# Two graph layers on one core: the third hop computed in seven products, its weights applied behind it, and the tests of the matrix moved into layer 0's norm

## The chip, the cores and the metric

The kernel runs on one core of one Trainium2 chip. The metric is the device time of one execution in microseconds (us). Before the change it is 839.94 us, the median of three runs (839.57 to 840.18).

A core has a matrix engine, TensorE (PE), that multiplies a loaded 128-row block of weights (the first operand, `lhsT`) by columns that stream past it (`rhs`) and adds up in PSUM; it has VectorE (DVE), ScalarE (ACT) and GpSimd (POOL) for elementwise work between PSUM and SBUF, and SyncE (SP), which here only issues transfers (DMA). Each engine runs its own queue of instructions in order; semaphores join them.

## What is computed

```python
# x: (8, 2048, 64), adj: (2048, 2048): a symmetric 0/1 pattern with ones on the
# diagonal and about 0.4% of the rest set, each row divided by its sum
def layer0(x, A, embedding, weight, bias):            # D = 16, K = 3
    w = jnp.einsum('nd,dkio->nkio', embedding, weight)   # weights of each node
    b = jnp.einsum('nd,do->no', embedding, bias)
    As = [I, A, 2.0 * (A @ A) - I]
    x_g = jnp.einsum('knm,bmc->bnkc', jnp.stack(As, 0), x)
    return jnp.einsum('bnki,nkio->bno', x_g, w) + b
def layer1(x0, A, weight, bias):                      # both supports are adj
    x1 = A x0;  x2 = 2.0 * (A x1) - x0
    return concat([x0, x1, x2, x1, x2]) @ weight + bias  # weight: (320, 64)
x = layernorm(x + layer0(x, adj, ...))
x = layernorm(x + layer1(x, adj, adj, ...))
```

So the large work is four multiplications of the 2048 x 2048 matrix by 2048 x 512 features (8 batches of 64 channels), called hops here: two in layer 0, two in layer 1.

## The kernel before

**Tiles.** The 2048 nodes are NT = 16 tiles of P = 128. A tile of features is 128 x 512 (`z[s][t]`). `z[0]` holds x, later layer 0's output h; `z[1]` and `z[2]` hold what the hops give and what they add to.

**The matrix as a pattern.** Every row of `adj` has one value wherever it is not zero. The hops therefore multiply the 0/1 pattern [...]and scale the result by that value (`rcol`, `rrow`). A slab is 128 rows of `adj`, loaded by `slab` (L191) on SP's queue, which carries the loads in program order into RAW = 5 rotating buffers `raw`; `places` (L196) makes the pattern on DVE. `places_equal` (L201) makes it too, and counts in the same instruction (L205) how many elements equal the row's value. `check` (L648) compares that count with the count of elements that are not zero (L445, an ACT copy `seen` with an accumulator, in the first hop); if they differ, `general`, a kernel for any matrix, computes the output in place of this one. Features are split in two fp32r parts, `high` (L208, ACT) and `low` (L211, DVE), so every product is two matmuls.

**First hop** (`hop_x`, L396; about 6 to 122 us). 512 matmuls of 512 columns (L229). `put_together` (L386) makes sums of quarters of the pattern on the side and POOL's queue writes them to DRAM (`sums_of`, L394).

**Second hop** (`seven_products`, L460; to 225 us). Seven products of half-size matrices in place of eight, with those sums: 7 x 8 steps of 8 matmuls of 512 columns, 448 in all (L529). The features are the loaded operand and the pattern streams past, so the result comes out transposed, into `z2`, by `put` (L545). Where a product needs a plain quarter of the pattern, it is loaded as a slab and made by `places`; products 2 to 4 read `sums_of`.

**Layer 0's mixing** (L623 to L640; 226 to 593 us). For each tile `mix0` (L321) has eight groups of 12 matmuls `pm` (L342); DVE adds each group into `acc`, scaled by the node's embedding, with four instructions of 128 x 256 (L348). `layernorm` (L303) follows: sum over channels (L306) and times 1/64 (L307) on DVE, subtraction on POOL (L309, `xc`), squares on ACT (L300), their sums on DVE (L301), `rsqrt` (L278), and the product on POOL (L312). `project` (L353) multiplies the transposed h by three 64 x 64 weights `v` (L361, 192 columns at a time), copies two of the results with ACT (L368) and adds the bias to the third with DVE (L369). The loop overlaps tiles: ahead of tile t's last group, `between` (L628) transposes h of tile t - 1 (L268, L270), prepares tile t + 1's operands (a load of `xt`, and transposes) and scales tile t + 2 (`times_r`, POOL); `project` of tile t - 1 stands behind tile t's groups.

**Third hop** (`hop_h`, L600; 593 to about 711 us). Pattern times h, after the projection: 16 slabs for 4, 8 and 4 tiles, 512 matmuls (L229), each slab made by `places_equal`, so that the whole matrix is tested here; results are scaled and added to `z[1]` by `evict` (L252), whose weights h already carries through `project`.

**Fourth hop** (`hop_g`, L675, and `hop_tile`, L697). Pattern times `z[1]`: the first eight tiles together, slab by slab in the order `ks`, then tiles 8 to 15 one by one, each normalised and stored (L318, L319) as it ends. PE ends at 826.9 us.

**What sets the order.** PSUM is one pool of four buffers of two banks each (`bank`, L81), which all of the above take in turn; a matmul into a buffer waits for the last reader of what was there four takings ago. Instructions wrapped in `ordered` keep the program's order while `in_order` is set, which it is during the first two hops and from the middle of the third hop's beginning on; elsewhere, in the mixing stage above all, a scheduler places them by readiness. `run` (L236) takes a list of steps, each made of parts with a lead (operands two steps ahead of their use, and so on), and pops two entries of `todo` (evictions and the like) per step.

Of the kernel before, what the change touches and what calls it, by code (L numbers as in the profile page):

```python
# [37 lines left out]
def pattern(  # L38
# [20 lines left out]

    nc = tc.nc  # L60
# [13 lines left out]
    rowpool = pool(hops, "frow", 1, side="right")  # L74
    hpool = pool(hops, "fhl", HL, side="right")
# [37 lines left out]
    v = const.tile([P, 3, C], F32, tag="v", name="v")  # L113
# [122 lines left out]
    def run(steps):  # L236

        got = [{} for _ in steps]
        for i in range(-6, len(steps)):
            for ahead in range(6, -1, -1):  # L240
                for lead, part in steps[i + ahead] if 0 <= i + ahead < len(steps) else ():
                    if lead == ahead:
                        part(got[i + ahead])
            for _ in range(2):
                if todo and i >= 0:
                    todo.pop(0)()
# [15 lines left out]
    def transpose(src, tag, pt=None):  # L262

        pt = bank("pt") if pt is None else pt
        for j in range(B // 2):
            for h in range(2):
                q = slice(h * C, (h + 1) * C)
                nc.tensor.transpose(pt[:, h, j * C : (j + 1) * C], src[q, 2 * j * C : 2 * (j + 1) * C], ident[q, q])  # L268
        tt = work2.tile([P, B // 2, P], F32, tag=tag, name=tag)
        nc.scalar.copy(  # L270
            tt.rearrange("p j (h n) -> p h j n", h=2), pt[:, :, : B // 2 * C].rearrange("p h (j n) -> p h j n", n=C)
        )
        return tt
# [4 lines left out]
    def rsqrt(ss):  # L278


        def col(name):
            return (work if ss.shape[1] == B else keep).tile(list(ss.shape), F32, tag=f"{name}{ss.shape[1]}", name=name)

        va = col("ln_v")
        nc.vector.scalar_tensor_tensor(va, ss, 1.0 / C, eps.to_broadcast(list(ss.shape)), ALU.mult, ALU.add)
        sd = col("ln_sd")
        nc.scalar.activation(sd, ss, AF.Sqrt, bias=eps, scale=1.0 / C)  # L287
        r0 = col("ln_r0")
        nc.vector.reciprocal(r0, sd)

        q = col("ln_q")
        nc.vector.scalar_tensor_tensor(q, r0, -0.5, r0, ALU.mult, ALU.mult)
        nc.vector.tensor_tensor(q, q, va, ALU.mult)
        r = col("ln_r")
        nc.vector.scalar_tensor_tensor(r, q, 1.5, r0, ALU.add, ALU.mult)
        return r

    def square_sums(src, to):
        sq = work.tile([P, B, C], F32, tag="ln_sq", name="sq")
        nc.scalar.activation(sq, src, AF.Square)  # L300
        nc.vector.tensor_reduce(to, sq, AX.X, ALU.add)  # L301

    def layernorm(src):  # L303

        s = work.tile([P, B], F32, tag="ln_s", name="s")
        nc.vector.tensor_reduce(s, src, AX.X, ALU.add)  # L306
        nc.vector.tensor_tensor(s, s, part, ALU.mult)  # L307
        xc = xcpool.tile([P, B, C], F32, tag="ln_xc", name="xc")
        nc.gpsimd.tensor_tensor(xc, src, wide(s), ALU.subtract)  # L309
        ss = work.tile([P, B], F32, tag="ln_ss", name="ss")  # L310
        square_sums(xc, ss)
        nc.gpsimd.tensor_tensor(xc, xc, wide(rsqrt(ss)), ALU.mult)  # L312
        return xc
# [7 lines left out]
    def mix0(t, tt, between):  # L321
# [4 lines left out]
        for g in range(2):  # L326
            part = acc[:, 4 * g : 4 * g + 4, :]
            nc.gpsimd.tensor_tensor(  # L328
# [3 lines left out]
            )  # L332
            for dg in range(D // DG):
                if g == 1 and dg == D // DG - 1:
                    between()
# [10 lines left out]
                for d in range(DG):  # L346
                    dd = dg * DG + d
                    nc.vector.scalar_tensor_tensor(  # L348
                        part, pm[:, :, :, d, :].rearrange("p j i c -> p (j i) c"), emb_sb[:, t, dd : dd + 1], part, ALU.mult, ALU.add
                    )  # L350
        return layernorm(acc)

    def project(t, hT, pus=None):  # L353


        for g in range(2):
            pm = bank("pu") if pus is None else pus[g]
            for i in range(2):
                for j in range(2):
                    q = slice(j * C, (j + 1) * C)  # L360
                    nc.tensor.matmul(  # L361
                        pm[:, j, i * 3 * C : (i + 1) * 3 * C], lhsT=hT[q, 2 * g + i, :], rhs=v[q],
                        start=True, stop=True,
                    )
            got = pm[:, :, : 6 * C].rearrange("p j (i k c) -> p j i k c", i=2, k=3)
            bs = slice(4 * g, 4 * g + 4)
            for s in range(2):
                nc.scalar.copy(bc(s, t)[:, bs, :].rearrange("p (i j) c -> p j i c", j=2), got[:, :, :, 2 - s, :])  # L368
            nc.vector.tensor_tensor(  # L369
                bc(2, t)[:, bs, :].rearrange("p (i j) c -> p j i c", j=2), got[:, :, :, 0, :],  # L370
                bias1.unsqueeze(1).unsqueeze(1).to_broadcast([P, 2, 2, C]), ALU.add,
            )
# [10 lines left out]
    S1, S2, S4, S3 = range(4)  # L383
    couple = []
# [11 lines left out]
    def hop_x(g, kk, j):  # L396
# [37 lines left out]
        def use(got):  # L434
# [10 lines left out]
            ordered(nc.scalar.activation(seen, s, AF.Copy, accum_out=nonzero[:, i : i + 1]))  # L445
            if last and g == 1:
# [13 lines left out]
    def seven_products(s, to, more):  # L460
# [3 lines left out]
        sums, kept = [], {}  # L464

        def sum_of_y(kk, name):
# [11 lines left out]
            if name == "T2":  # L478
# [4 lines left out]
                return add(y, add(y, quarter(2, 2), quarter(1, 2), ALU.subtract), quarter(1, 1), ALU.add)  # L483
            y = xcpool.tile([P, BC], F32, tag="ln_xc", name="y")
            if name == "T4":
                return add(y, kept[kk // 2][:, kk % 2], quarter(2, 1), ALU.subtract)
# [3 lines left out]
        def step(p, kk):  # L490
# [5 lines left out]
            def y_high(got):  # L496
                hl = hpool.tile([P, 2, BC], F32R, tag="hl", name="hl")
                got["hl"] = [hl[:, 0], hl[:, 1]]
                if name[0] == "B":
                    sum_y(got)  # L500
# [5 lines left out]
            def load_sum(got):  # L506
                if isinstance(which, tuple):
                    return
                raw = got["raw"] = rawp.tile([P, 2, Q], BF16, tag="raw", name="raw")
                load(nc.sync, raw, sums_of[kk, :, :, which, :].rearrange("g m n -> m g n"))  # L510

            def operands(got):
                if isinstance(which, tuple):
                    got["s"] = places(slab(kk + KK * which[1], which[0] * HALF, HALF))
# [7 lines left out]
            def use(got):  # L522
# [10 lines left out]
                if p == 0 and kk == 3:  # L533
                    node_bias(sums[1])
                    todo.extend(lambda h=h: keep_node_bias(sums[1], h) for h in range(2))
                if kk < KK - 1:
                    return
                if p < 6:
                    todo.extend([lambda: None] * 4)
                for i in range(2):  # L540
                    for c in range(2):
                        todo.append(lambda i=i, c=c: put(acc[i][:, c], i, c))
                todo.extend(more.get(p, ()))
# [21 lines left out]
            before = [(5, sum_y)] if name[0] != "B" else []  # L565
# [8 lines left out]
    def times_r(t):  # L574
# [6 lines left out]
    pieces = weights()  # L581
    more = {
        1: [lambda: ordered(next(pieces)) for _ in range(13)],
        5: [lambda: times_r(0), lambda: times_r(1)],
    }
    run([hop_x(g, kk, j) for g in range(2) for kk in range(KK) for j in range(2)] + seven_products(1, to_z2, more))
# [13 lines left out]
    def hop_h(g, first, n, k):  # L600
        def operands(got):
            if g == 0 and k == NT - 1:
                project(mixed[0], transpose(mixed[1].rearrange("p b c -> p (b c)"), "hT"))
                layer0.close()
                in_order.append(True)
            i = g * NT + k
            raw = slab(k, first * P, n * P)
            got["s"], got["hl"] = places_equal(raw, first * P, equal[:, i : i + 1]), halves(z[0][k])

        def use(got):  # L610
            s, hl = got["s"], got["hl"]
            if k == 0:
                accs[:] = banks(n)
            add_block(accs, s, hl, k == 0, k == NT - 1)
            if k == NT - 1:
                for i, a in enumerate(accs):
                    evict(z[1][first + i], first + i, a, i % 2)

        return [(2, operands), (0, use)]

    third = [hop_h(g, first, n, k) for g, (first, n) in enumerate(((0, 4), (8, 8), (4, 4))) for k in range(NT)]

    mixed = None  # L623
    tt = operands(0)
    for t in range(NT):
        done = {}

        def between():  # L628
            if mixed is not None:
                done["hT"] = transpose(mixed[1].rearrange("p b c -> p (b c)"), "hT")  # L630
# [5 lines left out]
        new = t, mix0(t, tt, between)  # L636
        tt = done.get("tt")
        if mixed is not None:
            project(mixed[0], done["hT"])
        mixed = new  # L640
# [7 lines left out]
    def check():  # L648
# [3 lines left out]
        tc.keep_in_program_order(nc.vector.tensor_tensor(bad, count("n_nz", nonzero), count("n_eq", equal), ALU.not_equal))  # L652
# [15 lines left out]
    EARLY = 8  # L668
    late = []
    ks = [0, 1, 2, 3, 8, 9, 10, 11, 12, 13, 14, 15, 4, 5, 6, 7]  # L670
    hls = {}
    sums = keep.tile([P, 8, B], F32, tag="sums", name="sums")
    late_values = {}

    def hop_g(k):  # L675
        def operands(got):
            i = ks.index(k)
            if i == EARLY:
                hops.close()
            if i in (0, EARLY):  # L680
                late.append(pool(ctx, f"flate{i}", 1, reuse_waits="tile"))
            got["s"] = places(slab(k, 0, HALF))
# [3 lines left out]
        def use(got):  # L686
            s, hl = got["s"], hls[k]
            if k == ks[0]:
                accs[:] = banks(8)
            add_block(accs, s, hl, k == ks[0], k == ks[-1])  # L690
            if k == ks[-1]:
                for t, a in enumerate(accs):
                    evict(z[2][t], t, a, t % 2)

        return [(2, operands), (0, use)]

    def hop_tile(t, c):  # L697
        def operands(got):
# [3 lines left out]
            got["s"] = places(raw)  # L702

        def use(got):
# [13 lines left out]
            for o in (2 * t - 16, 2 * t - 15):  # L718
                if o < 8:
                    square_sums(bc(2, o), sums[:, o, :])  # L720
            if t == 11:
                late_values["scales"] = rsqrt(sums.rearrange("p t b -> p (t b)"))
            if t >= 12:
                for o in (2 * t - 24, 2 * t - 23):
# [9 lines left out]
    run(third + [hop_g(k) for k in ks] + [hop_tile(t, c) for t in range(8, NT) for c in range(2)])  # L734
# [324 lines left out]
```

## Time and profile before

| what | before |
|---|---|
| median of 3 runs | 839.94 us |
| the profiled execution | 839.63 us |
| its span (first to last instruction) | 837.6 us |
| granted PE clock, mean | 0.994 |
| busy: PE, DVE, ACT, POOL | 823.5, 607.0, 224.6, 128.8 us |
| moved by DMA | 96.55 MB, 115 GB/s in the mean |

The page in front of all gives each engine's busy time and share of the span. Below it the span is cut into 40 equal slices, whose digits are busy tenths (9 is 90% or more). Then come the chain of work that ended last, followed back from the last instruction, and the costliest groups of instructions: line, engine, operation, result and operands by the program's names, shape, count; behind the bar the busy time, the mean of one in ns, and the idle time ahead of them with what ended most of it. A timeline lists one engine's instructions as start, duration (both us), engine, line, operation, operands, shape, count of a run of equal ones, and in brackets an idle time ahead and what ended it. PE's weight loads (PEld) are listed apart from its matmuls, which they overlap.

### The profile page before, as it was taken

How to read it: one execution, taken by the hardware profiler on the slowest of the kernel's cores; microseconds unless marked ns; L12 is line 12 of the kernel's file. 1: busy time of each engine (PE TensorE's matmuls, PEld its weight loads, DVE VectorE, ACT ScalarE, POOL GpSimd, SP SyncE). 2: the span in 40 equal slices, each digit the busy share in tenths (PEclk: the TensorE clock that was granted, in tenths of full speed). 3: DMA queues.
4: the chain of work that ended last, by engine and by line, in shares of the span. 5: the costliest groups of instructions: out<-in, count | busy, mean ns of one | idle time of the engine just before them, and what ended most of it. 6: DMA issues, size and time to landing. Idle time of an engine off the chain costs nothing.

```text
span 837.6 us, 14392 instructions
## 1 busy us (share of the span) xinstructions
PE 823.5 (98%) x5614; PEld 732.0 (87%) x5614; DVE 607.0 (72%) x1256; ACT 224.6 (27%) x427; POOL 128.8 (15%) x130
## 2 busy tenths in 40 slices
PE   9999999999999999999999999989999999999995
PEld 6888888888888999999999999989888878888884
DVE  6868657757878888888788888897867567534662
ACT  5436445772002111111111111101331132401210
POOL 0100000002731111111111111020101020102133
PEclk9999999999999999999999999999999999999998
DMA  9976775558200000000000000120256227544462
GB/s 332 394 273 221 248 258 174 154 163 289 88 14 14 11 6 13 14 14 13 14 14 13 14 14 14 42 86 2 76 182 190 94 74 240 173 142 126 132 183 92
DMA packets 57180, 96.55 MB, mean 115 GB/s; under 512 B 3984, under 2 KB 28816, under 8 KB 56976
## 3 DMA queue, kind: packets, MB, share of 16 engines
q1 hardware_dynamic: 52208, 82.69, 30.6%
q0 software_dynamic: 2304, 8.39, 3.0%
q10 hardware_dynamic: 2592, 4.47, 1.5%
q8 instruction: 47, 0.77, 0.4%
q14 instruction: 29, 0.24, 0.1%
HBM read 82.94 MB, written 12.58 MB: 114 GB/s over the span
## 4 chain that ended last, share of the span: by engine, by line
PE 93%; DVE 4%; issue 1%; DMA 0%; ACT 0%; POOL 0%; SPq 0%; DVEq 0%; POOLq 0%
PE pm L342 36%; PE acc L229 35%; PE accT L529 12%; PE a L229 7%; DVE acc L348 3%; PE pu L361 2%; PE pt L268 1%; PE first L133 1%; DVE s L205 0%; DMA raw<-in_adj 0%; POOL got L318 0%; DVE s L306 0%; ACT L287 0%; PE accT L144 0%; POOL xc L309 0%
## 5 line engine op out<-in xcount | busy, mean ns | idle before, releaser
L229 PE MATMUL acc<-hl,s 128*128 128x512 f32 x1280 | 292.7, 390 | 0.3 <-DVE acc L348 0.3
L229 PEld LDWEIGHTS acc<-hl,s 128*128 128x128 f32 x1280 | 239.4, 188 | 52.9 <-issue 1.2
L348 DVE SCALAR_TENSOR_TENSOR acc<-pm,pack_sb,acc 128x256 f32<-128x256 f32 x512 | 246.3, 483 | 43.5 <-PE pm L342 21.1
L342 PE MATMUL pm<-w,xt 64*128 64x256 f32 x1024 | 161.1, 379 | 3.1 <-DVE acc L348 2.8
L342 PE MATMUL pm<-w,z 64*128 64x256 f32 x1024 | 160.4, 378 | 0.0
L342 PE MATMUL pm<-w,t 64*128 64x256 f32 x1024 | 160.1, 377 | 0.2 <-ACT t L270 0.2
L342 PEld LDWEIGHTS pm<-w,xt 64*128 64x128 f32 x1024 | 108.1, 188 | 5.6 <-issue 1.8
L342 PEld LDWEIGHTS pm<-w,t 64*128 64x128 f32 x1024 | 110.7, 188 | 2.0 <-ACT t L270 0.6
L342 PEld LDWEIGHTS pm<-w,z 64*128 64x128 f32 x1024 | 110.8, 188 | 1.4
L198 DVE TENSOR_SCALAR s<-raw 128x1024 fp32r<-128x1024 f32 x87 | 68.1, 783 | 57.8 <-PE acc L229 48.8
L529 PE MATMUL accT<-s,hl 128*128 128x512 f32 x448 | 102.0, 389 | 0.0
L529 PEld LDWEIGHTS accT<-s,hl 128*128 128x128 f32 x448 | 84.0, 188 | 17.5
L209 ACT CAST hl<-z 128x512 fp32r<-128x512 f32 (+1 forms) x120 | 67.0, 578 | 119.1 <-PE acc L229 108.5
L213 DVE TENSOR_TENSOR hl<-z,hl 128x512 fp32r<-128x512 f32 (+1 forms) x120 | 81.5, 681 | 13.6 <-ACT hl L209 10.7
L205 DVE SCALAR_TENSOR_TENSOR s<-raw,rrow 128x512 fp32r<-128x512 f32 (+1 forms) x48 | 45.8, 956 | 26.7 <-PE acc L229 25.3
L270 ACT COPY hT<-pt 128x512 f32<-128x512 f32 x16 | 9.4, 586 | 204.4 <-PE pt L268 204.4
L309 POOL TENSOR_TENSOR xc<-acc,s 128x512 f32<-128x512 f32 x16 | 17.1, 1068 | 282.4 <-DVE s L307 282.4
L229 PE MATMUL a<-hl,s 128*128 128x512 f32 x256 | 58.5, 390 | 0.0
L229 PEld LDWEIGHTS a<-hl,s 128*128 128x128 f32 x256 | 48.0, 188 | 10.0
L258 POOL TENSOR_TENSOR z<-z,got 128x512 f32<-128x512 f32 x12 | 18.8, 1592 | 155.2 <-ACT got L257 155.1
L328 POOL TENSOR_TENSOR acc<-z,ebias 128x256 f32<-128x256 f32 x32 | 27.0, 866 | 87.1 <-ACT hl L209 85.6
L517 ACT CAST s<-raw 128x1024 fp32r<-128x1024 bf16 x32 | 33.6, 1050 | 10.6 <-ACT hl L209 10.6
(87 smaller groups left out, 477.0 us busy)
## 6 DMA issues: line engine op xcount, KB each, us to landing
raw<-in_adj SPq DMA_DIRECT2D x103, 512.0 KB, 4.5
raw<-in_adj SPq DMA_DIRECT2D x34, 256.0 KB, 3.0
sums_of<-z POOLq DMA_DIRECT2D x16, 512.0 KB, 4.9
raw<-sums_of SPq DMA_DIRECT2D x32, 256.0 KB, 2.8
xt<-in_xT SPq DMA_DIRECT2D x16, 256.0 KB, 2.7
out<-got ACTq DMA_DIRECT2D x16, 256.0 KB, 2.0
z<-in_x SPq DMA_DIRECT2D x15, 256.0 KB, 9.3
w<-in_w SPq DMA_DIRECT2D x3, 512.0 KB, 5.8
```

What stands on the lines that cost most here:

```text
L198: ordered(nc.vector.tensor_scalar(s, raw, 0.0, None, ALU.not_equal))
L205: ordered(nc.vector.scalar_tensor_tensor(s, raw, 0.0, r, ALU.add, ALU.is_equal, accum_out=count))
L209: ordered(nc.scalar.copy(to[0], src))
L213: ordered(nc.vector.tensor_tensor(to[1], src, to[0], ALU.subtract))
L229: nc.tensor.matmul(accs[i], lhsT=s[:, i * P : (i + 1) * P], rhs=hl[h], start=(first and h == 0), stop=(last and h == 1),)
L258: ordered(nc.gpsimd.tensor_tensor(to, to, got, ALU.add))
L309: nc.gpsimd.tensor_tensor(xc, src, wide(s), ALU.subtract)
L328: nc.gpsimd.tensor_tensor(part.rearrange("p (j i) c -> p j i c", j=2), bc(0, t)[:, 4 * g : 4 * g + 4, :].rearrange("p (i j) c -> p j i c", ...
L342: nc.tensor.matmul(pm[:, j, i], lhsT=tt[k][q, 2 * g + i, :], rhs=w[k][q, ds, :], start=(k == 0), stop=(k == 2),)
L348: nc.vector.scalar_tensor_tensor(part, pm[:, :, :, d, :].rearrange("p j i c -> p (j i) c"), emb_sb[:, t, dd : dd + 1], part, ALU.mult, ALU.add
L517: ordered(nc.scalar.copy(s, got["raw"]))
L529: nc.tensor.matmul(acc[i][:, c], lhsT=hl[h][:, i * P : (i + 1) * P], rhs=S[:, c * 512 : (c + 1) * 512], start=(kk == 0 and h == 0), stop=( ...
```

## The change

**Third hop.** `hop_h` goes. The third hop is `seven_products` again, on h itself instead of the projected h: 448 matmuls of 512 columns instead of 512. Its result, transposed, goes to new tiles `zT`. The third weight is applied behind it: `weigh` multiplies `zT` by `v[:, 2]` in fp32 matmuls of 64 columns, 128 in all (32 in each of products 5 and 6 of the hop, 16 in each of four steps of the next hop), and `add_weighed` adds the results to `z[1]` with DVE. `project` now handles two weights: 128 columns at a time instead of 192, and one ACT copy per half instead of two.

**Plain quarters of the pattern.** ACT writes each `seen` of the first hop (128 x 1024, bf16) to DRAM (`quarters`); in the second and third hop the three late products that need a plain quarter read it from there instead of loading a slab and making `places`. Only product 1 still does the latter.

**Tests.** With `hop_h` the tests of the whole matrix go. Its second column half is now tested by `test(k)` in the mixing loop: one 128 x 1024 instruction for each tile, in place in the slab's buffer, written into the program between the norm's subtraction and its squares, for tile t slab t; slab 15's test stands in tile 8's loop. Columns 0 to 767 are tested by `places_equal` in `hop_g`, and columns 768 to 1023 in the first two tiles of `hop_tile`.

**Layer 0's norm** is a generator that pauses after the subtraction, the squares and the root; around the test its parts keep the program's order. It writes h to `z[0]`, with the batches in another order, so that `project`'s results come out in whole blocks.

**Last tile.** Tile 15's mixing is in program order throughout; the operands of the third hop's first two steps are placed between its groups (`early`), the projection of tile 14 too, and the transposes and the projection of tile 15 stand in the third hop's first product.

**Fourth hop.** Six tiles together and ten one by one, instead of eight and eight; slabs in natural order.

**Pools.** `frow`, `fhl` and `v` live to the end of the kernel; the change is described as putting operands at equal addresses modulo 64.

```diff
     def layernorm(src, to):
...
+        ordered(nc.vector.tensor_reduce(s, src, AX.X, ALU.add))
+        ordered(nc.vector.tensor_tensor(s, s, part, ALU.mult))
         xc = xcpool.tile([P, B, C], F32, tag="ln_xc", name="xc")
+        ordered(nc.gpsimd.tensor_tensor(xc, src, wide(s), ALU.subtract))
+        yield
+        sq = squares(xc)
+        yield
...
+        ordered(nc.vector.tensor_reduce(ss, sq, AX.X, ALU.add))
...
     def project(t, hT, pus=None):
...
-                        pm[:, j, i * 3 * C : (i + 1) * 3 * C], lhsT=hT[q, 2 * g + i, :], rhs=v[q],
+                        pm[:, j, i * 2 * C : (i + 1) * 2 * C], lhsT=hT[q, 2 * g + i, :], rhs=v[q, 0:2, :],
...
     def hop_x(g, kk, j):
...
+            if j == 1:
+                ordered(nc.scalar.dma_start(out=quarters[kk, :, :, g, :], in_=seen))
...
     def seven_products(s, to, sums, more, wait=4):
...
-                    got["s"] = places(slab(kk + KK * which[1], which[0] * HALF, HALF))
+                if which == (0, 0):
+                    got["s"] = places(slab(kk, 0, HALF))
...
+    def weigh(ts, pairs, bs):
+        for n, t in enumerate(ts):
+            to = columns(pairs, n, bs)
+            for i in range(2 * len(bs)):
+                for j in range(2):
+                    q, block = slice(j * C, (j + 1) * C), 2 * bs[0] + i
+                    nc.tensor.matmul(
+                        to[:, j, i * C : (i + 1) * C], lhsT=zT[t // 8, t // 4 % 2][q, t % 4, block * P : (block + 1) * P],
+                        rhs=v[q, 2, :], start=True, stop=True,
+                    )
...
+    third = seven_products(0, to_zT, sums3, {
+        (0, 4): [last_transposed],
+        (0, 6): [last_projected],
+        4: half_weighed(1, 0), 5: half_weighed(0, 1),
+    }, wait=2)
...
+    def test(k):
+
+        raw = slab(k, HALF, HALF)
+        return lambda: tc.keep_in_program_order(
+            nc.vector.scalar_tensor_tensor(
+                raw, raw, 0.0, rrow[:, HALF:], ALU.add, ALU.is_equal, accum_out=equal[:, k : k + 1]
+            )
+        )
+
     tt = operands(0)
     for t in range(NT):
...
+        at = {(1, 3): [between]}
+        if t == NT // 2:
+            at[1, 2] = [test(NT - 1)]
+        if t == NT - 1:
+
+            in_order.append(True)
+            at = {
+                (0, 1): [lambda: early(0)], (0, 3): [lambda: early(1)], (1, 0): [between],
+                (1, 1): [lambda: project(t - 1, done["hT"])],
+            }
+        norm = mix0(t, tt, at)
+        next(norm)
+        if t == NT - 1:
+            todo.extend(lambda: next(norm) for _ in range(3))
+            break
+        in_order.append(True)
+        test(t)()
+        next(norm)
+        next(norm)
+        in_order.clear()
+        next(norm)
         tt = done.get("tt")
+        if t > 0:
+            project(t - 1, done["hT"])
```

## The prediction

> **What bounds the kernel now.** I read the page first, then the chain that ended last, then the timeline of VectorE (DVE), GpSimd (POOL) and TensorE (PE) inside layer 0's mixing stage. The page's engine shares and the chain's shares:
>
> ```profile
> span 837.6 us, 14392 instructions
> PE 823.5 (98%) x5614; PEld 732.0 (87%) x5614; DVE 607.0 (72%) x1256; ACT 224.6 (27%) x427; POOL 128.8 (15%) x130
> PE 93%; DVE 4%; issue 1%; DMA 0%; ACT 0%; POOL 0%; SPq 0%; DVEq 0%; POOLq 0%
> ```
> and from the list of groups by shape, the tests of the third hop:
> ```profile
> L205 DVE SCALAR_TENSOR_TENSOR s<-raw,rrow 128x1024 fp32r<-128x1024 f32 x16 | 20.6, 1288 | 15.5 <-PE acc L229 15.5
> ```
>
> TensorE is the bound almost everywhere: 512 matmuls of the first hop take 116.62 us in the chain, 0.2278 each. But an average hides the mixing stage (226 to 593 us). There DVE is as long as PE. DVE's timeline for one tile:
>
> ```profile
> 495.85 2.04 DVE L348 SCALAR_TENSOR_TENSOR acc<-pm,pack_sb,acc 128x256 f32<-128x256 f32 x4 [0.92 <-PE pm L342]
> 497.81 0.41 DVE L369 TENSOR_TENSOR z<-pu,pack_sb 128x256 f32<-128x256 f32 x1
> 498.14 0.68 DVE L306 TENSOR_REDUCE s<-acc 128x8 f32<-128x512 f32 x1
> 498.85 0.17 DVE L307 TENSOR_TENSOR s<-s,part 128x8 f32<-128x8 f32 x1
> 498.93 0.42 DVE L369 TENSOR_TENSOR z<-pu,pack_sb 128x256 f32<-128x256 f32 x1
> 500.89 0.69 DVE L301 TENSOR_REDUCE ss<-sq 128x8 f32<-128x512 f32 x1 [1.54 <-ACT sq L300]
> 502.78 14.73 DVE L348 SCALAR_TENSOR_TENSOR acc<-pm,pack_sb,acc 128x256 f32<-128x256 f32 x28
> 518.42 2.04 DVE L348 SCALAR_TENSOR_TENSOR acc<-pm,pack_sb,acc 128x256 f32<-128x256 f32 x4 [0.91 <-PE pm L342]
> ```
>
> A tile is eight product groups pm; four PSUM buffers rotate, and counting back (pm, pt, pt) the last group takes the buffer of the sixth, so it waits until DVE has accumulated the sixth. The loop: last accumulate starts 495.85; L307 ends 499.02 (3.17 later); L301 starts 500.89 (1.87); next tile's accumulates start 502.78 (1.89); six groups end about 515.36 (12.58); PE starts the last group 515.54 (0.18; 0.15 in tiles where PE is seen waiting); DVE starts on it 2.88 later. Sum 22.57 with 0.18, 22.54 with the binding 0.15. PE's own tile work is 2.65 + 18.13 (products) + 1.30 (L361) + 0.49 (transposes) = 22.57. So DVE has 0.03 us to spare. The tile before the last proves the loop; POOL and DVE there, each from its timeline:
>
> ```profile
> 546.12 0.69 DVE L205 SCALAR_TENSOR_TENSOR s<-raw,rrow 128x512 fp32r<-128x512 f32 x1
> 546.77 1.49 DVE L205 SCALAR_TENSOR_TENSOR s<-raw,rrow 128x512 fp32r<-128x512 f32 x1
> ```
> ```profile
> 521.73 1.04 POOL L309 TENSOR_TENSOR xc<-acc,s 128x512 f32<-128x512 f32 x1 [17.71 <-DVE s L307]
> 546.28 1.43 POOL L309 TENSOR_TENSOR xc<-acc,s 128x512 f32<-128x512 f32 x1 [19.70 <-DVE s L307]
> ```
>
> A test (L205) stands directly behind L307; it starts 0.16 us before POOL's subtraction L309, which then takes 1.43 instead of 1.04 and ends 0.90 behind the test's end; the next test, caught behind L309, takes 1.49 instead of 0.69. DVE's chain grew by 1.98 + 1.29 us there, and PE's last group came 25.81 us after the previous one (538.11 to 563.92) instead of 22.57: +3.24. Added DVE time reaches PE whole.
>
> **What the Trainium skill says.** "SBUF — State Buffer", Who interferes with whom: a DVE instruction with two SBUF inputs and a GpSimd instruction that reads SBUF exclude each other; the second to issue waits. The 1.43 and 1.49 above agree. "TensorE: Matmul & The Clock Gate", Architectural detail: DVE and ACT are strict FIFO, so nothing overtakes a waiting L301; DVE's order in the timeline agrees. Same page, LDWEIGHTS: a load takes its 128 columns / 1.2, 107 ns, whatever the rows. The trace's 32 loads of L144 (fp32, 64 columns moved, four row groups) take 0.98 us, the last 0.19: seven steps of 0.113 us between sets, twice what 64 columns would need at L342's rate (0.108 x 64/256 x 2 = 0.054); it agrees. Same page, What's actually happening: after a mostly idle window of about 3.4 us PE gets half its clock. The trace has it once: behind the 1.68 us stall before 563.92 matmuls take 1.13 instead of 0.63 and 24 of them 4.52 us instead of 2.65.
>
> **The change, part by part.**
> *Third hop, 64 matmuls fewer.* 512 become 448 (7 products x 8 x 8): -64 x 0.2278 = -14.6 us. On the path.
> *Weights behind it.* New: 128 fp32 matmuls of 64 columns (2 x 32 in products 5 and 6, 4 x 16 in the next hop), two records each, two row groups side by side: 128 sets. No row shows this form. Upper price 0.113 (L144's spacing: the load binds), lower 0.062 (transposes L268, 16 in 0.49 us, two side by side); below nothing is excluded, PE must issue them and nothing else runs. I take 0.113: L144 is the same kind of matmul, a transpose another. +14.4 us (low 7.9). It eats the hop's saving.
> *Projection 192 to 128 columns.* 1.30 x 128/192 = 0.87 us, by the load bound 8 x 0.113 = 0.90: -0.4 a tile on PE, but worth nothing while DVE sets the pace. The two ACT copies dropped per tile are not on the path.
> *Tests inside the norm.* By the built order DVE now runs, per tile: three accumulates, L369, the fourth, L369, L306, L307, test (128x1024), L301. The second L369 stood in the wait for ACT before; now it is ahead of L306. Spacings (acc to acc 0.52, acc to L369 0.40, L369 to next 0.33) give 3.38 instead of 3.17: +0.21. The test waits for a transfer issued a tile earlier, so it starts as the L205 did, ahead of L309, and lasts 1.22 (undisturbed 128x1024 instances of L205 in the timeline; the 1288 above includes caught ones). L309 then ends at -0.02 + 1.22 + 0.90 = 2.10 us behind L307 instead of 1.18: +0.92, and ACT's square, L301 and all behind them shift. Bounds for this shift: 0 if the cover (1.54 us idle above) held it, 0.45 if POOL went first, 0.92 if DVE does; I take 0.92. New loop 22.54 + 0.21 + 0.92 = 23.67 us, +1.10. Queued behind: everything on DVE; PE waits 1.5 us before its last group. The test of tile 15 inside tile 8 costs about 0.3 (1.2 on DVE, mostly beside PE). First period 22.16 + 0.92. So the last group of tile 14 starts at 244.49 + 23.08 + 13 x 23.67 + 0.3 = 575.6 instead of 563.92: +11.7, with the old stall of 3.24 already out. The 16 test loads (512 KB) and xt loads share SP's queue, which moves 13 GB/s there: nothing.
> *Last tile in order.* From that group on, before: 28.7 us to the third hop (593.01, less 0.46 for two early matmuls). After: accumulates start 11.1 us in; two operand pairs (1.2 each) are cut into them; by the rotation the fifth group waits for the second's accumulates (16.45 instead of 14.1) and the second pu buffer for the fourth's (21.85 instead of 19.5); third hop starts after 30.1, and its third step waits for L306, L307, two L213 and a places: 1.3. Sum 31.4: +2.7.
> *Last tile's transposes and projection*: 0.39 + 1.50 become 0.25 + 0.90: -0.7.
> *Quarters through DRAM.* 16 slab tests on DVE (0.78) become ACT casts (1.05 beside a 0.40: 1.45 of a 1.82 us step), hidden under PE; if not, up to 1 us at the last products. 16 stores of 256 KB on ACT's queue add 4.2 MB to a stage at 297 GB/s mean, peak 394: hidden, at worst 2 us of late operands at the start.
> *Later hop, 6 + 10 tiles instead of 8 + 8*: still 512 matmuls; DVE 1.61 of 2.73 us a step: nothing.
> *Equal addresses modulo 64.* In both built programs all large operands already start at 32 modulo 64: nothing.
>
> Sum: 11.7 + 2.7 - 14.6 + 14.4 - 0.7 = +13.5. The profiled execution's 837.6 span becomes 851.1, its 839.63 becomes 853.1; the median 839.94 lies 0.3 above: **853.4**.
>
> **Rivals.**
> A, faster (chance 0.13): the test hides in the 1.54 us wait without holding up POOL, and weights cost 0.062 a set. It decides at L309: if that still takes 1.04, the period is 22.54, the last tile's two parts become -4.0 and +1.6, sum -4.0 + 1.6 - 14.6 + 7.9 - 0.7 = -9.8: 830.1; with weights at 0.113 still 836.6. For it: the idle wait is there. Against: 1.43 above.
> B (0.22): PE's 1.5 us wait together with 0.49 us of transposes makes windows half idle, and the clock halves in about half of the tiles: 7 x 1.5 + 1.7 = +12: 865.6. For it: the one stall of 1.68 us did it. Against: 0.7 us before 266.65 did not.
> C (0.16): one of the unknown prices is at its low end: POOL first (-0.47 x 14 = -6.6) or cheap weights (-6.5): about 846.8.
> D (0.05): both at their low ends: 840.3, within 0.2%, the least that measurement tells from no change.
> My sum has 0.44. It is the likeliest, so 853.4 stands; the range 839 to 866 leaves out A and the far end of B. Faster 0.13, same 0.05, slower 0.82.
>
> **What would show it.** L309 at about 1.9 us and period 23.7 in tiles 1 to 13 with PE waiting on DVE before the last group: the test step right; 1.04 and 22.5: wrong. New weight matmuls 14 us in all: right; 8: wrong. accT of the third hop 102 us. A clock under 0.99 in the stage: B. If the period is right and the total not, the fault lies in the last tile or the start.

## The result and the profile after

The changed kernel takes 865.44 us (median of 4 runs, 865.3 to 865.78) against 840.06 us for the kernel before on the same chip (839.57 to 840.52): a ratio of 1.0303, 95% interval 1.0285 to 1.0321. It is slower by 25 us, nearly twice the 13.5 that the sum gave. The page after, shares and chain:

```profile
span 863.7 us, 14822 instructions
PE 829.2 (96%) x5806; PEld 727.9 (84%) x5806; DVE 608.1 (70%) x1311; ACT 267.5 (31%) x464; POOL 121.3 (14%) x121
PE 68%; DVE 22%; issue 5%; POOL 3%; ACT 1%; DMA 1%; DVEq 0%; POOLq 0%
```

The chain tells the new bound: DVE's share went from 4% to 22% and POOL's from 0 to 3%, nearly all in the mixing. DVE's timeline for the tile that the prediction showed of before:

```profile
512.36 1.52 DVE L367 SCALAR_TENSOR_TENSOR acc<-pm,pack_sb,acc 128x256 f32<-128x256 f32 x3 [0.90 <-PE pm L361]
513.80 0.41 DVE L389 TENSOR_TENSOR z<-pu,pack_sb 128x256 f32<-128x256 f32 x1
514.13 0.47 DVE L367 SCALAR_TENSOR_TENSOR acc<-pm,pack_sb,acc 128x256 f32<-128x256 f32 x1
514.52 0.41 DVE L389 TENSOR_TENSOR z<-pu,pack_sb 128x256 f32<-128x256 f32 x1
514.85 0.68 DVE L318 TENSOR_REDUCE s<-acc 128x8 f32<-128x512 f32 x1
515.56 0.17 DVE L319 TENSOR_TENSOR s<-s,part 128x8 f32<-128x8 f32 x1
515.65 1.22 DVE L715 SCALAR_TENSOR_TENSOR raw<-raw,rrow 128x1024 f32<-128x1024 f32 x1
...
518.46 0.69 DVE L326 TENSOR_REDUCE ss<-sq 128x8 f32<-128x512 f32 x1 [1.59 <-ACT sq L309]
...
520.34 14.73 DVE L367 SCALAR_TENSOR_TENSOR acc<-pm,pack_sb,acc 128x256 f32<-128x256 f32 x28
535.97 1.00 DVE L367 SCALAR_TENSOR_TENSOR acc<-pm,pack_sb,acc 128x256 f32<-128x256 f32 x2 [0.90 <-PE pm L361]
```

POOL in that tile, and TensorE at its last group:

```profile
515.88 1.89 POOL L321 TENSOR_TENSOR xc<-acc,s 128x512 f32<-128x512 f32 x1 [17.97 <-DVE s L319]
```
```profile
533.07 0.70 PE L361 MATMUL pm<-w,xt 64*128 64x256 f32 x4 [1.24 <-DVE acc L367]
```

The test starts 0.23 us ahead of the subtraction, which takes 1.89 us instead of 1.04. DVE then idles 1.59 us for the squares: the wait that was to hide the test is as long as before, only later. From 512.36 to 535.97 is the loop: 23.61 us. TensorE waits 1.24 us in it.

What the sum did not have is in the hops. TensorE's groups by shape, of before and then of after (busy time, mean of one in ns):

```profile
L229 PE MATMUL acc<-hl,s 128*128 128x512 f32 x1280 | 292.7, 390 | 0.3 <-DVE acc L348 0.3
L529 PE MATMUL accT<-s,hl 128*128 128x512 f32 x448 | 102.0, 389 | 0.0
```
```profile
L560 PE MATMUL accT<-s,hl 128*128 128x512 f32 x896 | 210.5, 395 | 1.7 <-DVE s L199 1.7
L230 PE MATMUL acc<-hl,s 128*128 128x512 f32 x512 | 120.0, 396 | 0.2 <-ACT hl L210 0.2
L230 PE MATMUL a<-hl,s 128*128 128x512 f32 x320 | 74.1, 392 | 0.0
L670 PE MATMUL accT<-v,zT 64*128 64x64 f32 x256 | 15.6, 274 | 0.0
```

The first hop is the same work for TensorE in both, with waits of 0.2 us in all, and one of its matmuls lasts 396 ns; in the group of before that holds it the mean is 390. From start to start that is 232.4 instead of 226.9 ns in the mean of the steady steps. The mixing's matmuls of 256 columns keep their spacing (107.9 ns in both) and the granted clock is 0.996. The way of the time, each stretch read between the same events of the two traces:

| stretch | before | after | difference | forecast |
|---|---|---|---|---|
| start to tile 0's last group | 244.49 | 251.00 | +6.5 | 0 |
| from there to tile 14's last group | 319.43 | 329.29 | +9.9 | +11.7 |
| to the third hop's first matmul | 29.09 | 30.83 | +1.7 | +1.4 |
| to the last matmul's start | 235.07 | 242.46 | +7.4 | +0.4 |
| to the end | 9.5 | 10.1 | +0.6 | 0 |

For before the third hop counts from 593.01 us, where it runs on after two early matmuls at 592.02 us; the forecast of +1.4 took their 0.46 us off. The last matmul of before starts at 828.08 us, later than the end of 826.9 that the text on the kernel before gives.

### The profile page after: what moved, and what is told of

The parts are those of the page before. It is cut to its first block, busy times and chain, and to the rows that moved or that the text cites. A ratio compares the mean times of both kernels' runs of the same rounds, so it can differ in the third digit from the quotient of the medians.

```text
span 863.7 us, 14822 instructions
## 1 busy us (share of the span) xinstructions
PE 829.2 (96%) x5806; PEld 727.9 (84%) x5806; DVE 608.1 (70%) x1311; ACT 267.5 (31%) x464; POOL 121.3 (14%) x121
## 3 DMA queue, kind: packets, MB, share of 16 engines
q1 hardware_dynamic: 63920, 86.88, 31.4%
## 4 chain that ended last, share of the span: by engine, by line
PE 68%; DVE 22%; issue 5%; POOL 3%; ACT 1%; DMA 1%; DVEq 0%; POOLq 0%
PE accT L560 23%; DVE acc L367 18%; PE pm L361 17%; PE acc L230 14%; PE a L230 6%; PE accT L230 5%; POOL xc L321 2%; PE accT L670 2%; DVE ss L326 1%; DVE s L318 1%; DVE z L389 1%; ACT sq L309 1%; DMA z<-in_x 1%; PE pu L380 1%; POOL got L337 0%
## 5 line engine op out<-in xcount | busy, mean ns | idle before, releaser
L560 PE MATMUL accT<-s,hl 128*128 128x512 f32 x896 | 210.5, 395 | 1.7 <-DVE s L199 1.7
L560 PEld LDWEIGHTS accT<-s,hl 128*128 128x128 f32 x896 | 168.2, 188 | 41.9 <-ACT sq L309 1.8
L230 PE MATMUL acc<-hl,s 128*128 128x512 f32 x512 | 120.0, 396 | 0.2 <-ACT hl L210 0.2
L230 PEld LDWEIGHTS acc<-hl,s 128*128 128x128 f32 x512 | 96.0, 188 | 24.4 <-DVE z L452 1.1
L548 ACT CAST s<-raw 128x1024 fp32r<-128x1024 bf16 x96 | 100.8, 1050 | 48.4 <-ACT hl L210 36.3
L214 DVE TENSOR_TENSOR hl<-z,hl 128x512 fp32r<-128x512 f32 (+1 forms) x96 | 53.4, 562 | 34.4 <-ACT hl L210 31.7
L321 POOL TENSOR_TENSOR xc<-acc,s 128x512 f32<-128x512 f32 x16 | 29.0, 1810 | 284.6 <-DVE s L319 284.6
L210 ACT CAST hl<-z 128x256 fp32r<-128x256 f32 (+1 forms) x96 | 47.5, 510 | 64.7 <-PE acc L230 28.7
L230 PE MATMUL accT<-hl,s 128*128 128x512 f32 x192 | 45.4, 394 | 0.0
L230 PEld LDWEIGHTS accT<-hl,s 128*128 128x128 f32 x192 | 35.8, 188 | 8.0
L467 ACT ACTIVATE seen<-s 128x1024 bf16<-128x1024 f32 x32 | 33.7, 1054 | 18.6 <-DMA quarters<-seen 18.6
```

Of the source, the lines that this page charges most:

```text
L210: ordered(nc.scalar.copy(to[0], src))
L214: ordered(nc.vector.tensor_tensor(to[1], src, to[0], ALU.subtract))
L230: nc.tensor.matmul(accs[i], lhsT=s[:, i * P : (i + 1) * P], rhs=hl[h], start=(first and h == 0), stop=(last and h == 1),)
L321: ordered(nc.gpsimd.tensor_tensor(xc, src, wide(s), ALU.subtract))
L548: ordered(nc.scalar.copy(s, got["raw"]))
L560: nc.tensor.matmul(acc[i][:, c], lhsT=hl[h][:, i * P : (i + 1) * P], rhs=S[:, c * 512 : (c + 1) * 512], start=(kk == 0 and h == 0), stop=( ...
```

## Experiments

**The two addresses of a matmul.** The start addresses are read from the built programs; no trace holds them. Before, the moving operand (the one that streams) and the stationary one (the loaded one) of every matmul of the hops start at 480 modulo 512 bytes. After, the pools on one side of SBUF lie 384 bytes further (`v` adds 768 bytes to `fkeep`, the norm of six tiles in place of eight takes 384 off), and 1664 of the 1920 pair 352 with 480. Inside the trace after, the other 256 (352 with 352) have a spacing of 227.4 ns, the 1664 of 232.4. To test it, 128 unused bytes went ahead of the pools that follow, in the changed kernel and in the one before:

```diff
     ident = keep.tile([P, P], F32, tag="ident", name="ident")
+    keep.tile([P, 32], F32, tag="pad", name="pad")
```

> The changed kernel with 128 bytes of unused SBUF put ahead of its left-hand pools, so that both operands of every matmul of the hops start at 480 modulo 512 (as built, 1664 of 1920 pair 352 with 480). Theory (the pair of addresses sets the rate): all of these matmuls fall from 232.5 to 227 ns, 1664 x 5.5 ns = 9.2 us, so about 856.3 us. Rival (the added traffic through DRAM or the longer lists of instructions slow TensorE): spacing stays at 232 ns and the time at 865.4.

Measured: 857.61 us, ratio 1.0219 (1.0202 to 1.0236); spacing 227.0 ns everywhere.

> The kernel before with the same 128 bytes: 1472 of its 1984 matmuls of the hops now pair 96 with 480 modulo 512, the last 512 have equal addresses. Theory (addresses): those 1472 go from 227 to 232.5 ns, +8.1 us, 848.2 us, the last two stages stay at 227. Rival (something else in the changed kernel): 840.1 and 227 ns everywhere.

Measured: 847.91 us, ratio 1.0104 (1.0087 to 1.0121). The page of this run shows it in one view, the unequal pairs and the last stage with equal ones:

```profile
L530 PE MATMUL accT<-s,hl 128*128 128x512 f32 x448 | 104.5, 395 | 0.0
L230 PE MATMUL a<-hl,s 128*128 128x512 f32 x256 | 58.5, 390 | 0.0
```

The spacing is 232.4 ns for the 1472 unequal pairs, whichever operand is the shifted one, and 227.0 for the rest. So in both kernels these matmuls become slow or fast by the addresses alone. In the padded changed kernel the profiled span falls by 7.7 us and not 9.0 (1664 x 5.4 ns), and 1.0 of the 7.7 is only a first matmul that starts earlier (5.55 us against 6.58). The second hop and all from the third hop on are shorter by what the spacing gives (2.5 and 3.8 us), but the first hop by 0.4 in place of 2.8. TensorE now meets a wait there, where the changed kernel's slower steps were only stretched by 0.6:

```profile
66.40 1.81 PE L231 MATMUL acc<-hl,s 128*128 128x512 f32 x5 [1.68 <-DVE z L453]
```

DVE takes the first column half out of PSUM late (L453, after four sums L416). The slow addresses had hidden this.

Which difference counts? The kernel before with other pads:

> The kernel before with 64 bytes of padding: 1472 matmuls of the hops pair 32 with 480 modulo 512, equal modulo 64 but not modulo 128; the last 512 pair 32 with 32. If addresses must agree modulo 128: 232 ns or more for the 1472. If modulo 256 alone counts (a difference of exactly 128 is what hurts): 227.

> The kernel before with 256 bytes of padding: 1472 matmuls of the hops pair 224 with 480 modulo 512, equal modulo 256 but not modulo 512. If addresses must agree modulo 256: 227 ns throughout and 839. If they must agree modulo 512 or more: about 232 ns for the 1472 and 847.

> The kernel before with 32 bytes of padding: 1472 matmuls of the hops pair 0 with 480 modulo 512, a difference of 32 bytes. If any difference below the modulus slows them: 229 to 233 ns and 842 to 847. If only differences of 64 or 128 bytes do: 227 and 839.

Measured, one execution each: with 64 bytes 845.47 us, spacing 233.3 ns where the stationary operand is shifted and 228.9 where the moving one is; with 32 bytes 846.92 us and 233.4 ns both ways; with 256 bytes 837.53 us and 226.9 ns, as without a pad. The same group of the page with 256 bytes:

```profile
L530 PE MATMUL accT<-s,hl 128*128 128x512 f32 x448 | 102.0, 389 | 0.0
```

So start addresses that are equal modulo 256 are fast, and differences of 32, 64 and 128 bytes are not; equality modulo 64 is not enough. Other differences were not tried. That 837.53 lies 2.1 us under the profiled 839.63 of before is not the pad's work. In the profiled execution of before the granted clock is 0.5 from 564.96 to 568.37 us, behind the wait of 1.68 us in the mixing. With 32, 64 and 256 bytes of padding that wait is there too (1.69 us with 64 bytes), but the clock stays whole behind it, and the stretch from tile 14's last group to the third hop is 1.7 us shorter. So the same wait halves the clock in one execution and not in another.

**The test in the norm.** First its place, then its kind:

```diff
-        if t == NT // 2:
-            at[1, 2] = [test(NT - 1)]
+        at[1, 2] = [test(t)]
+        if t == NT // 2:
+            at[1, 2].append(test(NT - 1))
...
-        test(t)()
         next(norm)
```

> The changed kernel with each tile's test placed ahead of the accumulates of the seventh product group, where the test of slab 15 already stands in tile 8, instead of behind the subtraction of the norm. Theory (the test holds up POOL, L321 1.89 us): L321 falls to 1.04, the loop to 22.54 + 0.21 + 0.16 = 22.9 us instead of 23.61, over 14 periods -9.8, and +1.0 for the two tests of tile 8: about 856.6 us. Rival 1 (the longer loop is the moved L389 and the fixed order of the norm, not the test): L321 1.04 but the loop 23.4 or more, 863 or more. Rival 2 (time on DVE counts whole wherever it stands): 23.97 a tile, about 870.

Measured: 857.06 us, ratio 1.0213 (1.0193 to 1.0232); loop 22.92 us. POOL and DVE in the tile of above:

```profile
509.03 1.04 POOL L321 TENSOR_TENSOR xc<-acc,s 128x512 f32<-128x512 f32 x1 [18.13 <-DVE s L319]
```
```profile
502.23 1.22 DVE L715 SCALAR_TENSOR_TENSOR raw<-raw,rrow 128x1024 f32<-128x1024 f32 x1
503.37 0.08 DVE L715 DVE_READ_ACCUMULATOR raw<-raw,rrow 128x1 f32 x1
503.37 3.67 DVE L367 SCALAR_TENSOR_TENSOR acc<-pm,pack_sb,acc 128x256 f32<-128x256 f32 x7
```

The test lasts 1.22 us as before, but DVE no longer waits 0.90 us for TensorE's last group behind it: all but about 0.15 us of it is free here (the loop is 22.92 us, against 22.77 in the next experiment, where the test is hidden).

```diff
-            nc.vector.scalar_tensor_tensor(
-                raw, raw, 0.0, rrow[:, HALF:], ALU.add, ALU.is_equal, accum_out=equal[:, k : k + 1]
+            nc.vector.tensor_scalar(
+                raw, raw, 0.0, 0.0, ALU.not_equal, ALU.add, accum_out=equal[:, k : k + 1]
```

> The changed kernel with the tests as an operation with one SBUF input (it counts what is not zero and leaves the comparison with the row's value out), at the same places in the order. Theory (two SBUF inputs exclude POOL's reads): L321 1.04, the test ends before the squares arrive and is hidden, loop 22.54 + 0.21 = 22.75 instead of 23.61, about 853.4 us. Rival 1 (any test of this length there delays POOL or the norm): L321 stays at 1.9 and the time at 865. Rival 2 (it is DVE's time itself): loop 23.6, 865.

Measured: 853.14 us, ratio 1.0173 (1.0156 to 1.019); loop 22.77. DVE and POOL, the operation as long as the test and in the same place:

```profile
528.35 1.21 DVE L715 TENSOR_SCALAR_CACHE_REDUCE raw<-raw 128x1024 f32<-128x1024 f32 x1
529.49 0.08 DVE L715 DVE_READ_ACCUMULATOR raw<-raw 128x1 f32 x1
530.32 0.69 DVE L326 TENSOR_REDUCE ss<-sq 128x8 f32<-128x512 f32 x1 [0.75 <-ACT sq L309]
```
```profile
528.58 1.04 POOL L321 TENSOR_TENSOR xc<-acc,s 128x512 f32<-128x512 f32 x1 [17.97 <-DVE s L319]
```

It ends 0.75 us before the squares come: hidden. So neither DVE's time nor the fixed order lengthened the norm, but the second SBUF input of the test. The remaining 0.2 us over before fits the 0.21 forecast for the second L389, which stands ahead of the sums now; no run moved it back.

**The weights.** The loops of `weigh` run over nothing, and `add_weighed` returns at once.

```diff
-        for n, t in enumerate(ts):
+        for n, t in enumerate(()):
...
     def add_weighed(ts, n, pairs, bs):
+        return
```

> The changed kernel without the third weight behind the third hop (weigh and add_weighed issue nothing, so that term of layer 1 is left out). Theory (all 128 sets lie on TensorE's path and cost 0.118 each, as the trace has them, 15.2 us in all): 865.4 - 15.2 = 850.2 us. Rival (part of their time is a wait for operands that stays): 855 or more. Rival (they cost more than their own time, because evictions stand in the way): 848 or less.

Measured: 848.92 us, ratio 1.012 (1.0103 to 1.0137). From 1.0303 that is 0.0183 x 838.8 = 15.4 us, by the two intervals give or take 2. The traces say it more closely: from the first matmul of the third hop to the last of all it is 242.46 us with the weights and 226.12 without, so they cost 16.3 us. Their own time is 15.2, whole on the path; the rest comes at the six places where TensorE goes over to them and back, where the neighbouring matmuls take about 0.2 us longer together. In a row, two of them side by side come every 112 ns, and so do those of `project` with twice the columns (128): here the columns do not set the price.

**All repairs together**, the pad, the tests' place and this:

```diff
-            ordered(nc.gpsimd.tensor_tensor(
+            nc.gpsimd.tensor_tensor(
                 part.rearrange("p (j i) c -> p j i c", j=2),
```

> The changed kernel with three repairs at once: 128 bytes ahead of the left-hand pools (all operands of the hops at 480 modulo 512), the tests ahead of the seventh group's accumulates, and the start of tile 15's accumulator no longer held in program order behind the end of tile 14's norm on POOL. If the three causes are separate and add up: 865.4 - 9.2 (addresses, less 1.4 where the last stage was fast already is in it) - 8.8 (tests) - 1.9 (first accumulate of tile 15) = 845.5 us, still slower than before by what the weights cost beyond the 14.6 us of the hop, the later L389 and the last tile's order. Rival (they cover one another): 850 or more. Rival (the third hop's seven products are worth what they save): below 840.

Measured: 845.32 us, ratio 1.0075 (1.0063 to 1.0088). The causes add up to within a microsecond or so (the pad alone had given 7.8 of its 9.2 us), and what is left is slower than before. The third hop now starts 28.17 us behind tile 14's last group instead of 30.83.

**A version that beats both.** What was learnt of the waits, applied to the kernel before: its stall in tile 13 comes from four tests of the third hop in the norm. Each goes ahead of the seventh group's accumulates of one of the tiles 12 to 15, so into DVE's wait for the eighth and last group (the accumulates of these tiles are kept in program order), and `hop_h` uses what was made. Tile 13, counted from 0, is the one that the prediction calls the tile before the last.

```diff
+                if g == 1 and dg == D // DG - 2 and t >= NT - 4:
+                    early(t - NT + 4)
...
+    def early(k):
+        raw = slab(k, 0, 4 * P)
+        in_order.append(True)
+        tested[k] = places_equal(raw, 0, equal[:, k : k + 1])
+        in_order.clear()
```

> The kernel before with the first four tests of the third hop, which stand in tile 13's norm, put one each into the wait of DVE for the last product group of tiles 12 to 15. Theory (a test is free there and costs its time and POOL's delay in the norm): the loop's 3.24 us of tile 13 to 14 and the halved clock behind it go, 840 - 3.2 - 1.9 + 0.3 for the third hop's start = 835 us. Rival (DVE's time counts wherever it stands): 840 - 3.2 + 4 x 0.7 = 839.6.

Measured: 834.82 us, ratio 0.9952 (0.994 to 0.9964): 4.0 us under the 838.82 of before on the same occasion, and about 30 under the change. DVE in tile 13:

```profile
537.67 0.68 DVE L205 SCALAR_TENSOR_TENSOR s<-raw,rrow 128x512 fp32r<-128x512 f32 x1
538.28 0.08 DVE L205 DVE_READ_ACCUMULATOR s<-raw,rrow 128x1 f32 x1
538.28 2.04 DVE L351 SCALAR_TENSOR_TENSOR acc<-pm,pack_sb,acc 128x256 f32<-128x256 f32 x4
540.82 2.04 DVE L351 SCALAR_TENSOR_TENSOR acc<-pm,pack_sb,acc 128x256 f32<-128x256 f32 x4 [0.50 <-PE pm L344]
```

A test of 0.68 us takes its time out of a wait of 0.9, of which 0.50 is left; the loop stays at 22.57, and the 3.24 us of the stall are gone. How much the clock adds cannot be told from this run, since before has its halved time in some executions only.

## Why the prediction was right, and where it was not

The direction and its first cause were right; the size was half. That the time still lies inside the range of 839 to 866 is luck: the upper end was meant for a halved clock, which did not come. By its own steps:

- *Tests inside the norm.* Right: L321 1.89 us (about 1.9 forecast), loop 23.61 (23.67), and two experiments that put the cause on the exclusion. What was said of added DVE time in general, that it reaches PE whole, holds for this place and not for every place: PE's last group waits for the accumulates of the sixth, and a test behind those cost 0.15. "SBUF — State Buffer", Who interferes with whom, also says that a DVE instruction with at most one SBUF input, outside the modes that use two ports, does not contend with GpSimd; the run with one input agrees, 1.04. The stage came out 1.8 under the forecast: in tile 0 the subtraction ran ahead of the test (1.04 us), so the first period did not grow, the loop was 0.06 shorter 13 times, and slab 15's test cost 0.16, not 0.3.
- *Weights behind it.* The price of a set was right: 15.2 us in the trace (0.118 a set; 0.113 taken). The changes to them and back were not in the sum; with these they cost 16.3, 1.9 more than forecast. They give back more than the third hop saves.
- *Third hop, 64 matmuls fewer.* Right in number, but 448 at 232.4 ns save 12.1 us, not 14.6.
- *Equal addresses modulo 64: nothing.* **This step failed.** The prediction asked of the built programs only equality modulo 64, the modulus in the change's own words, and found it in both. The differing bits are just above: 1664 matmuls at 5.5 ns are 9.2 us, most of the 12 missing. About 5.3 of the first +6.5, 2.5 in the third hop and 1.4 in the fourth are this. "Later hop: nothing" fell with it.
- *Last tile in order.* Forecast 31.4 with the wait behind it; measured 30.83 + 1.38 + 0.28 = 32.5. The wait before the third step was foreseen (1.3). Not foreseen: tile 15's accumulator is started by POOL (L347) only behind the end of tile 14's norm (L331), so the first accumulate came 6.57 us behind the sums instead of the 4.61 of this kernel's other tiles; the repaired kernel has 3.76. The transposes and the projection behind it became 0.39 + 1.09 us, not 0.25 + 0.90.
- *Quarters through DRAM.* Nearly hidden as built: the steps around 66 us are 0.6 us longer. With equal addresses the first hop loses more there, a wait of 1.68 us in the padded kernel; no run separates the quarters from the rest of that stage. The first matmul also starts 0.70 us later (6.58 against 5.88), but in the other traces of the changed kernel it starts at 5.55 to 5.98, so this belongs to the one execution.
- *Rivals.* B gave 865.6, the time that was measured, for a reason that did not occur: the clock stayed at 0.996, with waits of 1.24 us in tile after tile. A time that agrees proves no mechanism; the loop and the clock, named ahead, do. A is out by L321, C and D by the weights and by L321.

Together the profiled span is 12.6 us over the sum's 851.1. Of these 9.2 are the addresses, 1.9 the weights, 1.1 the last tile, 0.7 the start, 0.5 the gaps in the first hop, 0.3 the last transposes and projection, 0.6 the end, and -1.8 the tests: 12.5. The 0.6 us at the end no run here explains.

## What to carry to other kernels

An idle wait hides an instruction only if what the engine waits for is not held up by that instruction: the same test cost 0.84 us in a wait of 1.6 us that POOL's subtraction had to end, and 0.15 in a wait of 0.9 us for TensorE. Work that is moved off a dense matmul into many narrow ones must be priced by their number and not by their columns: here 128 of 64 columns cost more than 64 of 512 save. And a change in pool sizes can be a change in addresses: compare the start addresses of matmul operands modulo 256 in the built programs before costing anything else.

## What the runs showed of the hardware

With fp32r operands of 512 columns (one record per matmul in the trace; the fp32 matmuls here leave two) and a fresh load for each matmul, the spacing is 226.9 ns where the moving and the stationary operand start at addresses equal modulo 256 (differences of 0 and 256 bytes), and 228.9 to 233.4 ns where they differ by 32, 64 or 128 bytes. With 128 bytes single spacings run from 228 to 241 ns, in a pattern that repeats every seven matmuls; in the fast case they are 226 or 227. "SBUF — State Buffer", Who interferes with whom, gives TensorE two independent read ports, one for each operand; the runs show that the spacing still depends on how the two start addresses lie to each other, by 2.4%. By what mechanism, no run here tells.
